# The local-attention mask as a ScalarE copy into PSUM, and K squared and rotated in two halves

## The chip, the cores and the metric

The kernel runs on one core of a Trainium2 chip. The metric is the device time of one execution in microseconds, as the median of several runs. TensorE appears in the profile as PE (its weight loads as PEld), VectorE as DVE, ScalarE as ACT, GpSimd as POOL and SyncE as SP. Arithmetic is float32 throughout, except for the mask products, which are bfloat16.

## The reference

The input x has 4 sequences of 512 tokens of width 128. First comes one global attention block with 16 heads of 64 (layer norm, causal penalty of -50, softmax, output product, residual). Then six layers follow, each made of a local attention and a feed-forward part, each with a residual. The part that matters here is the local attention of a layer:

```
qkv = shift_tokens(x) @ Wqkv             # 128 -> 3 x 1024
q = l2norm(q) * qs ; k = l2norm(k) * ksc
q = q*cos*scale + rotate_half(q)*sin*scale
k = k*cos/scale + rotate_half(k)*sin/scale
# windows of 32 queries; each sees its own 32 keys and the 32 before
mask = (it < jb) | (it > jb + w) | (jb == -1)
sim = where(mask, -max, 8 * q . k)
out = softmax(sim) @ v ;  return out @ Wo
```

The feed-forward part is a layer norm, a product of 128 to 2 x 341, a times GELU(gate), a product back to 128, with biases.

## The kernel before, in words

The program has two stretches. The first, to about 550 us, is the global attention; the change does not touch its work. The second handles the six layers as 96 **units** (6 layers x 4 sequences x 4 blocks of 128 tokens), and a **slot** per unit, in which three units are in progress at once: `u = unit(n)` gets its attention, `nxt = unit(n + 1)` its transposes, `new = unit(n + 2)` its projections, rotation and norms. The order of every engine's instructions is written out by hand in `slot` (L919); nothing is reordered, and each engine takes its own instructions in the order in which they stand there.

In a slot, in order of the program:

- `scores(u)` (L684): eight bfloat16 products of a 32-wide identity with the mask `band` (L690) start the two PSUM banks of the scores, 64 rows by 32 columns of the array each, 512 columns long. Then 64 small products q·k (L700; 128 matrix instructions, since a float32 product takes two passes) add to them. DVE takes the maximum (L710) and subtracts it (L712).
- The Q projection of `new` (L548), its square on ACT (L560); the exponentials of u on ACT (L718); for some slots a step of the layer norm; the output product of the unit before (L762); Q's rotation on DVE (L570, L576), added on POOL (L587).
- The K projection of `new` in two halves of 512 columns, each half in its own PSUM bank, between them the transposes of u's probabilities on PE (L661), each copied out by ACT (L664, pT). Then K's square on ACT in one instruction of 1024 columns (L560).
- `times_v(u, 0)` and `times_v(u, 1)` (L725): 32 small products each on PE (L737, 64 matrix instructions), then on DVE the division (reciprocal L746, product L747).
- K's rotation on DVE (L570, L576) and POOL's add (L587); the transpose of the output on DVE (L753); the sums of squares for Q and K (L565).
- `transpose_q(nxt)`: PE L661, ACT copies qT (L664). Then the V projection of `new` (L548), copied by ACT (L648, `keep_v`); `transpose_k(nxt)`: PE L661, ACT copies kT (L664).
- A step of the feed-forward part: two FFN products (L812, L813), a table load, GELU on ACT (L816), the gate on DVE (L820), or the closing product (L832, L835). Then the next slot's scores follow on PE. The inverse norms are taken on ACT and POOL (L590 to L603), and POOL applies them (L606).

The layer norm's and the feed-forward part's steps are spread over four slots each, so slots come in four kinds, by n modulo 4: without a norm step, with mean (L109), with variance (L118), with scale (L126). The feed-forward steps run from slot 7 on. In slots before that, K's transposes stand between the halves of the V projection. Once per 16 slots POOL also builds the rotation tables of a layer (L182).

PSUM for this stretch consists of three pairs of banks (`two_t`, L525), whose roles turn by one with every slot (`part[0] = -n % 3`), and two single banks (`one_t`). In a slot, pair 0 holds the scores, then the first half of PV, then V's projection; pair 1 holds Q's projection, then the second half of PV, then the FFN products; pair 2 holds K's projection, and turns into pair 0, the scores' pair, of the next slot. Squares and rotated products share four buffers (tag `t1`), the rotated vectors six (tag `rot`).

## Time and profile before

| what | us |
|---|---|
| median of 3 runs (lowest, highest) | 2070.51 (2067.06, 2072.57) |
| the profiled execution, its own time | 2072.4 |
| its span, first to last instruction | 2070.6 |
| PE busy | 2028.4 |
| DVE busy | 1640.8 |
| ACT busy | 1368.2 |
| POOL busy | 1316.5 |

The mean granted clock of TensorE is 0.996 of full speed. The engines run side by side, so their busy times do not add up; what counts is which engine is waited for. A line of the waits reads "engine and line waiting, engine and line waited for: us in total, times, longest". A line of the timeline reads "start, duration, engine, line of the code, operation, output <- inputs with their shapes, how many in a row", and in brackets the idle time ahead of it and who ended it. [...]

### The profile page before, as it was taken

The numbers are of one execution on the slowest core, as the hardware profiler recorded it, in microseconds if no ns is written. First come the engines' busy times: TensorE is split into PE (matmuls) and PEld (weight loads), VectorE is DVE, ScalarE is ACT, GpSimd is POOL, SyncE is SP. The second block draws the span as 40 slices with busy tenths as digits, with TensorE's granted clock in tenths as the row PEclk, the third lists the DMA queues.
The fourth block names the chain that finished last, engine by engine and source line by source line (L and its number), as shares of the span: only waits on it lengthen the run. The fifth ranks groups of instructions, "written<-read, shape, count | busy, mean of one in ns | idle before, by whom it ended". The sixth has DMA issues, their size and how long they took to land.

```text
span 2070.6 us, 77263 instructions
## 1 busy us (share of the span) xinstructions
PE 2028.4 (98%) x34382; PEld 1329.1 (64%) x34382; DVE 1640.8 (79%) x2240; ACT 1368.2 (66%) x2678; POOL 1316.5 (64%) x1432
## 2 busy tenths in 40 slices
PE   7999999999999999999999999999999999999998
PEld 5665555655466666666666666666666666666665
DVE  3766766767698888888888888888888888888885
ACT  3665665666455766676776676776667776677763
POOL 1554554555677677667767667667677767667762
PEclk8999999999999999999999999999999999999999
DMA  3000000000011121111211112111121111211110
GB/s 127 1 1 1 1 1 1 1 1 1 12 44 36 42 67 44 44 44 33 77 44 34 54 36 64 53 35 44 46 64 44 38 51 46 67 41 44 38 45 27
DMA packets 34968, 77.44 MB, mean 37 GB/s; under 512 B 4686, under 2 KB 18764, under 8 KB 34636
## 3 DMA queue, kind: packets, MB, share of 16 engines
q1 hardware_dynamic: 33932, 70.79, 11.8%
q8 instruction: 272, 4.46, 0.9%
q10 hardware_dynamic: 704, 1.70, 0.2%
q14 instruction: 60, 0.49, 0.1%
HBM read 23.50 MB, written 1.05 MB: 12 GB/s over the span
## 4 chain that ended last, share of the span: by engine, by line
PE 91%; DVE 5%; ACT 2%; POOL 1%; issue 1%; DMA 0%; SPq 0%; POOLq 0%; ACTq 0%
PE ps_proj L548 23%; PE ps_one L661 12%; PE ps_one L762 7%; PE ps_att L737 7%; PE ps_sc L308 6%; PE ps_o L393 6%; PE ps_att L700 5%; PE ps_pt L373 5%; PE ps_proj L812 3%; PE ps_proj L813 3%; PE ps_proj L832 3%; PE ps_pj L287 1%; PE ps_att L690 1%; PE ps_pj L277 1%; PE ps_pj L271 1%; PE ps_pj L407 1%
## 5 line engine op out<-in xcount | busy, mean ns | idle before, releaser
L587 POOL TENSOR_TENSOR rot<-rot,t 128x1024 f32<-128x1024 f32 x192 | 454.2, 2366 | 232.6 <-DVE t L576 220.1
L548 PE MATMUL ps_proj<-wqkv,xs 128*128 128x512 f32 x1152 | 569.0, 602 | 0.5 <-PE ps_one L661 0.2
L362 POOL TENSOR_TENSOR pr<-pr,den 128x1024 f32<-128x1024 f32 x128 | 241.0, 1893 | 248.3 <-DVE den L359 238.5
L606 POOL TENSOR_TENSOR rot<-rot,ss 128x1024 f32<-128x1024 f32 x192 | 361.3, 1903 | 7.4
L560 ACT ACTIVATE sq<-ps_proj 128x1024 f32<-128x1024 f32 x192 | 196.4, 1023 | 93.8 <-PE ps_proj L548 93.6
L548 PEld LDWEIGHTS ps_proj<-wqkv,xs 128*128 128x128 f32 x1152 | 188.2, 190 | 102.0 <-issue 92.1
L570 DVE TENSOR_TENSOR rot<-ps_proj,lt 128x1024 f32<-128x1024 f32 x192 | 233.3, 1215 | 10.2 <-ACT sq L560 10.0
L576 DVE TENSOR_TENSOR t<-ps_proj,lt 128x1024 f32<-128x1024 f32 x192 | 232.9, 1213 | 0.0
L348 ACT ACTIVATE pr<-ps_sc,nm 128x128 f32<-128x128 f32 (+3 forms) x448 | 220.3, 509 | 11.8 <-DVE nm L335 8.6
L565 DVE TENSOR_REDUCE ss<-sq 128x16 f32<-128x1024 f32 x192 | 221.1, 1190 | 0.0
L661 PEld LDWEIGHTS ps_one<-ident,rot 128*128 128x128 f32 x1536 | 172.7, 141 | 61.2 <-issue 51.2
L661 PE MATMUL ps_one<-ident,rot 128*128 128x128 f32 x1536 | 205.1, 276 | 1.1 <-POOL xs L170 0.6
L335 DVE TENSOR_REDUCE nm<-ps_sc 128x2 f32<-128x1024 f32 x128 | 155.9, 1218 | 62.9 <-PE ps_sc L323 62.8
L664 ACT COPY pT<-ps_one 128x512 f32<-128x512 f32 x192 | 110.0, 587 | 136.6 <-PE ps_one L661 136.6
L762 PEld LDWEIGHTS ps_one<-aT,wo 128*128 128x128 f32 x1536 | 182.9, 192 | 23.6 <-issue 17.7
L762 PE MATMUL ps_one<-aT,wo 128*128 128x128 f32 x1536 | 189.1, 276 | 0.3 <-ACT tmp_t L852 0.2
L746 DVE RECIPROCAL rden<-ps_att 128x8 f32<-128x8 f32 x192 | 38.8, 202 | 176.8 <-PE ps_att L737 176.7
L648 ACT COPY vt<-ps_proj 128x512 f32<-128x512 f32 x192 | 103.1, 590 | 96.4 <-PE ps_proj L548 96.4
L373 PEld LDWEIGHTS ps_pt<-ident,pr 128*128 128x128 f32 x1024 | 117.4, 142 | 58.5 <-issue 47.4
L664 ACT COPY qT<-ps_one 128x512 f32<-128x512 f32 x192 | 103.1, 589 | 66.1 <-PE ps_one L661 66.1
L377 ACT COPY pT<-ps_pt 128x512 f32<-128x512 f32 x128 | 75.6, 591 | 98.0 <-PE ps_pt L373 98.0
L373 PE MATMUL ps_pt<-ident,pr 128*128 128x128 f32 x1024 | 135.9, 274 | 3.0 <-DVE pT L381 2.4
(178 smaller groups left out, 3763.2 us busy)
## 6 DMA issues: line engine op xcount, KB each, us to landing
vs<-vt SPq DMA_DIRECT2D x96, 390.0 KB, 3.7
vs<-vt SPq DMA_DIRECT2D x72, 130.0 KB, 3.6
wqkv<-in_wqkv_dram SPq DMA_DIRECT2D x18, 512.0 KB, 4.0
vs<-in_zeros_dram SPq DMA_DIRECT2D x24, 130.0 KB, 3.7
wo<-in_wo_dram SPq DMA_DIRECT2D x6, 512.0 KB, 4.2
w<-in_w_dram SPq DMA_DIRECT2D x6, 341.0 KB, 5.9
xr<-in_x_dram SPq DMA_DIRECT2D x3, 256.0 KB, 7.6
scales<-in_scales_dram SPq DMA_DIRECT2D x6, 128.0 KB, 3.1
```

The costliest lines, as they stand in the source:

```text
L348: nc.scalar.activation(self.pr[:, h, cols], self.sc[:, h, cols], AF.Exp, bias=self.nm[:, part_, h : h + 1], accum_out=self.den[:, part_, h ...
L362: nc.gpsimd.tensor_tensor(self.pr, self.pr, self.den[:, 0].unsqueeze(2).to_broadcast([P, 2, S]), ALU.mult)
L373: nc.tensor.transpose(pt[:, k * P : (k + 1) * P], self.pr[:, h, k * P : (k + 1) * P], ident)
L548: mm(p[:, c, :], lhsT=u.xs[:, u.T * P : (u.T + 1) * P], rhs=wpart[j][:, c * 512 : (c + 1) * 512], start=True, stop=True,)
L565: nc.vector.tensor_reduce(u.ss[:, j * HEADS : (j + 1) * HEADS], heads(u.sq[j]), AX.X, ALU.add)
L570: nc.vector.tensor_tensor(heads(t0), heads(pf), lt[:, u.T, 2 * j].unsqueeze(1).to_broadcast([P, HEADS, HD]), ALU.mult)
L576: nc.vector.tensor_tensor(t1.rearrange("p (h t d) -> p h t d", t=2, d=half), pf.rearrange("p (h t d) -> p h t d", t=2, d=half)[:, :, ::-1, :],
L587: nc.gpsimd.tensor_tensor(u.r[j], u.r[j], u.t1, ALU.add)
L606: nc.gpsimd.tensor_tensor(heads(u.r[j]), heads(u.r[j]), u.ss[:, j * HEADS : (j + 1) * HEADS].unsqueeze(2).to_broadcast([P, HEADS, HD]), AL ...
L661: nc.tensor.transpose(tp[:, c * P : (c + 1) * P], src[:, (4 * g + c) * P : (4 * g + c + 1) * P], ident)
L664: nc.scalar.copy(dst[:, 4 * g : 4 * g + 4, col0 : col0 + P], tp.rearrange("p (c t) -> p c t", c=4))
L762: mm(y[:, 0:P], lhsT=wo_w[0][:, k, :], rhs=u.aT[:, g].rearrange("p (j f) -> p j f", f=P)[:, :, f0 : f0 + W], start=(k == 0), stop=(k == NC ...
```

## The change

For units 1 to 94 the mask no longer comes from products. At the end of the slot before, after the qT copies, ACT copies the mask (`mask`, a new float32 constant of 1 KB per partition, loaded at the start by one more DMA on SP's queue) into the pair of banks that K's projection has just left, broadcast over the eight chunks. The score products then add to it. Unit 0 and the last unit keep the products.

For that, K's banks must be read out earlier. In slots from 0 on, K's square is done in two halves of 512 columns, the first of them right behind the first half of K's projection, and K's rotation is done in halves as well: the first ahead of the first division, the second between the two divisions, where before it came after both. POOL's add for K follows the second half. `project` keeps K's pair of banks, unflattened, as `u.pk`.

```diff
+        nc.sync.dma_start(out=mask, in_=a["mask"])
         nc.sync.dma_start(out=tabs, in_=a["tabs"])
...
+    def square_half(u, c):
+        if c == 0:
+            u.sq[1] = s2a.tile([P, INNER], F32, tag="t1", name="sq", bufs=4)
+        nc.scalar.activation(u.sq[1][:, c * 512 : (c + 1) * 512], u.pk[:, c, :], AF.Square)
+
+    def rotate_half(u, c):
+        if c == 0:
+            u.r[1] = s2a.tile([P, INNER], F32, tag="rot", name="rot", bufs=6)
+            u.t1 = s2a.tile([P, INNER], F32, tag="t1", name="t1", bufs=4)
+        cols, lt, pf, half = slice(c * 512, (c + 1) * 512), u.lt, u.pk[:, c, :], HD // 2
+        nc.vector.tensor_tensor(
+            heads(u.r[1][:, cols]),
+            heads(pf),
+            lt[:, u.T, 2].unsqueeze(1).to_broadcast([P, HEADS // 2, HD]),
+            ALU.mult,
+        )
+        nc.vector.tensor_tensor(
+            u.t1[:, cols].rearrange("p (h t d) -> p h t d", t=2, d=half),
+            pf.rearrange("p (h t d) -> p h t d", t=2, d=half)[:, :, ::-1, :],
+            lt[:, u.T, 3].rearrange("p (t d) -> p t d", t=2).unsqueeze(1).to_broadcast([P, HEADS // 2, 2, half]),
+            ALU.mult,
+        )
...
+    def preset(u):
+        u.sc = two_t(2, "ps_att")
+        nc.scalar.copy(
+            u.sc.rearrange("p a (c n) -> p a c n", n=2 * W),
+            mask[:, min(u.T, 1)].unsqueeze(2).to_broadcast([P, 2, NC, 2 * W]),
+        )
+
     def scores(u):
-        sc = two_t(0, "ps_att")
-        for j, h, x_, p0 in PLACES:
+        sc = two_t(0, "ps_att") if u.sc is None else u.sc
+        for j, h, x_, p0 in PLACES if u.sc is None else ():
...
         if new:
             do_project(new, 1, 0, 1)
+            if n >= 0:
+                square_half(new, 0)
...
         if new:
             do_project(new, 1, 1)
-            square(new, 1)
+            if n == -1:
+                square(new, 1)
+            else:
+                rotate_half(new, 0)
+                square_half(new, 1)
...
         if u:
             times_v(u, 0)
+            if new:
+                rotate_half(new, 1)
+                add_rotated(new, 1)
             times_v(u, 1)
...
-        if new:
+        if new and n == -1:
             rotate(new, 1)
             add_rotated(new, 1)
...
         if nxt:
             transpose_q(nxt)
+        if new and n >= 0:
+            preset(nxt)
         if new:
             do_project(new, 2, 0, 2 if geglu else 1)
```

More of the change, by code (lines that the diff above doesn't have):

```diff
@@ L61, in body @@
     band = const.tile([P, 2, 2 * W], BF16, tag="band", name="band")
+    mask = const.tile([P, 2, 2, 2 * W], F32, tag="mask", name="mask")
     ident16 = const.tile([P, P], BF16, tag="ident16", name="ident16")
@@ L541, in __init__ @@
             self.i, self.b, self.T = i, b, T
-            self.r, self.sq = [None, None], [None, None]
+            self.r, self.sq, self.sc = [None, None], [None, None], None
     def project(u, j, c0=0, c1=2):
-        p = u.p[j] if c0 else two_t(((1, 2, 1), (0, 2, 1), (1, 2, 0))[min(u.n, 2)][j], "ps_proj")
+        p = (u.pk if j == 1 else u.p[j]) if c0 else two_t(((1, 2, 1), (0, 2, 1), (1, 2, 0))[min(u.n, 2)][j], "ps_proj")
         u.p[j] = p
+        if j == 1:
+            u.pk = p
         for c in range(c0, c1):
@@ L1141, in _constants @@
         band[r : r + W, 1] = np.where(seen, 0.0, NEG)
+    mask = np.repeat(band[:, 1:2, None, :], 2, 2).repeat(2, 1)
+    for r in range(0, P, HD):
+        mask[r + W : r + HD] = mask[r : r + W]
+        mask[r : r + W, 0, 0] = band[r : r + W, 0]
     band = band.astype(ml_dtypes.bfloat16)
@@ L1146, in _constants @@
     zeros = np.zeros((W, 2, NC, HD + 1), f)
-    return {"tabs": tabs, "band": band, "pen": pen, "ident16": ident16, "zeros": zeros}
+    return {"tabs": tabs, "band": band, "mask": mask, "pen": pen, "ident16": ident16, "zeros": zeros}
 def kernel(**inputs):
```

## The prediction

> **What bounds the kernel now.** I read the page's busy times and its chain first, then the waits, then the timeline of single slots, then the source lines of the mask products.

> ```profile
> PE 2028.4 (98%) x34382; PEld 1329.1 (64%) x34382; DVE 1640.8 (79%) x2240; ACT 1368.2 (66%) x2678; POOL 1316.5 (64%) x1432
> ...
> PE 91%; DVE 5%; ACT 2%; POOL 1%; issue 1%; DMA 0%; SPq 0%; POOLq 0%; ACTq 0%
> ```

> PE is busy 98% of the span, and 91% of the chain that ended last lies on it: a PE microsecond saved is worth one as long as nobody else becomes late. From the view of the waits:

> ```profile
> DVE rden L746 <- PE ps_att L737: 176.7, 98, 2.3
> ...
> ACT vt L648 <- PE ps_proj L548: 96.4, 95, 1.6
> ...
> PEld ps_one L661 <- ACT pr L718: 22.5, 35, 2.1
> ```

> The columns are total us, times, longest. DVE stands idle about 1.8 us (176.7/98) ahead of the first division of each slot, ACT about 1.0 us ahead of the V copies, both because PE is not there yet. PE itself waits for others mainly at one place, the transposes of the probabilities (L661), for the exponentials (L718).

> The timeline of one slot (start us, duration), the third of its group of four:

> ```profile
> 1207.03 1.02 PE L813 MATMUL ps_proj<-hT,w 128*85 128x512 f32 x2
> ...
> 1207.57 1.28 ACT L816 ACT_TABLE_LOAD   x1
> ...
> 1207.98 0.41 PE L690 MATMUL ps_att<-band,ident 64*32 64x512 bf16 x8
> ...
> 1208.21 1.46 PE L700 MATMUL ps_att<-kT,qT 64*32 64x64 f32 x128
> ...
> 1208.87 0.68 ACT L816 ACTIVATE tmp_t<-ps_proj,vecs 85x512 f32<-85x512 f32 x1
> ...
> 1209.58 0.75 DVE L820 SCALAR_TENSOR_TENSOR tmp_t<-ps_proj,vecs,tmp_t 85x512 f32<-85x512 f32 x1
> ...
> 1210.25 1.21 DVE L710 TENSOR_REDUCE mx<-ps_att 128x16 f32<-128x1024 f32 x1
> ...
> 1211.50 1.22 DVE L712 TENSOR_TENSOR pr<-ps_att,mx 128x1024 f32<-128x1024 f32 x1
> ...
> 1212.75 1.06 ACT L718 ACTIVATE pr<-pr 128x1024 f32<-128x1024 f32 x1
> ...
> 1214.10 0.60 PE L661 MATMUL ps_one<-ident,pr 128*128 128x128 f32 x4
> ...
> 1215.83 1.02 PE L548 MATMUL ps_proj<-wqkv,xs 128*128 128x512 f32 x2
> ...
> 1217.69 0.21 DVE L746 RECIPROCAL rden<-ps_att 128x8 f32<-128x8 f32 x1 [1.97 <-PE ps_att L737]
> ...
> 1218.92 1.07 ACT L664 COPY qT<-ps_one 128x512 f32<-128x512 f32 x2 [0.68 <-PE ps_one L661]
> ...
> 1221.08 1.07 ACT L648 COPY vt<-ps_proj 128x512 f32<-128x512 f32 x2 [1.08 <-PE ps_proj L548]
> ```

> Four things are to be seen: the eight mask products hold the score products back from 1207.98 to 1208.21; a serial chain runs from the V copies over table load, GELU, gate (L820), maximum, subtraction and exponentials to PE's transposes; DVE has a hole of 1.97 us before L746; ACT has one of 1.08 us before L648.

> **The change, part by part.**

> *Mask products off PE.* 94 of the 96 units (1 to 94) lose their eight products; unit 0 and the last keep them. From the first L690 to the first L700 it is 0.23 us; over all 96 slots of the trace the interval is 0.225 to 0.309 us and sums to 21.8 us. So 94/96 x 21.8 = 21.3 us go from PE. The 0.52 us between the starts of the last 128-row product and of the first L690 stays: PV products (L737), also in 64x32 tiles, stand 0.52 us behind L548 too.

> *Preset on ACT.* One copy of 128x1024 from SBUF into PSUM per slot. No row shows one. Bounds: 0.92 us (L560 to the next ACT start, 1228.06 to 1228.98) and 1.06 (mean of L718, SBUF to SBUF); I take 1.02, by L560 with the same shape between PSUM and SBUF. It stands behind the qT copies and ahead of V's, in the hole of 1.08 us that is there in all four kinds of slot. Two copies in a row overlap by about 0.1 us (two take 1.07 at 0.59 each), so it fits with 0.06 to 0.25 us over: cost nothing. Without that cover, V's copies and the chain behind them would come later by the excess. It also waits for DVE's last read of K's banks, below.

> *K by halves on ACT.* One 1.02 us square becomes two of 128x512: 0.59 (L664, same size) to 0.62 (L113). The second sits where the whole one did. The first comes before a pT copy: in the slot above K's first half is done for ACT at about 1215.60 (start of its second pass plus 0.63, as at 1216.26 to 1216.89), the half square runs to 1216.20, the copy that began at 1216.03 begins at about 1216.11, ends at 1216.70, and PE takes up PV at 1216.79: nothing. What queues behind it on ACT is the pT copy and then the second half square; PE waits for the copy, with 0.09 us left.

> *K by halves on DVE.* Two operations of 1.21 us (start to start 1.13) become four of 128x512 at 0.69 (L747, PSUM operand, same size), some 0.61 apart: 4 x 0.61 - 2 x 1.13 to 4 x 0.69 - 2 x 1.21, +0.18 to +0.34 us a slot, 17 to 32 us of DVE, none of it on the path. The first pair (1.30) starts after the first half square, 1216.26, and ends at 1217.56, ahead of the division at 1217.69; the four kinds of slot have holes of 1.56, 1.87, 1.97 and 2.02 us. The second pair starts when the first division's product (L747, 1217.93 to 1218.62) ends, and is through at 1219.84; ACT is free for the preset at 1219.9. The second division is 1.2 us later than now; its bank is next written by the FFN products, about 1 us later still. DVE then ends its sums of squares some 1.0 us earlier, but its next link, L820, waits for GELU, so this earns nothing in the steady slots. POOL's add for K starts earlier, with nobody waiting.

> *What is late next.* In the four kinds of slot the exponentials end ahead of PE's transposes by 0.25, 0.25, 0.29 and 0.06 us; where PE really waits (1261.49) the distance is 0.05. Slack is thus 0.20, 0.20, 0.24, 0.01. In the first three the chain begins at V's copies, before the mask products, and does not get shorter: 0.23 of PE time meets 0.20 of slack, so 0.03 comes back as waits in two kinds of slot, 48 x 0.03 = 1.4 us. In the fourth the chain starts at the Q projection, behind the scores, and moves with them: nothing. Once per 16 slots (table building on POOL, 5 times) PE already waits 0.8 us or more for a chain POOL-ACT two slots long (1244.48 to 1261.49); there both slots' 0.23 is lost: 5 x 0.45 = 2.3 us. In slots 1 to 7 there is no GELU and DVE itself is late; PE waits there beyond its usual spacing 3.2 us in all, and DVE's earlier end should give about 2 back.

> *Mask load.* One more transfer on SP's queue at about 16 us, ahead of the tables (L211, first used at 454.79): nothing.

> Sum: -21.3 + 1.4 + 2.3 - 2.0 = -19.6. Against the profiled execution (span 2070.6, 2072.4 with what lies around it) that is 2052.8; it stands 1.9 above the median of the runs, 2070.51, which gives **2051**.

> [...]

> **The rivals.**

> *K's second projection behind the half square (slower).* If the order is kept for K's whole tile and not for each bank, the product at 1215.83 waits for ACT's half square, 1216.20 plus 0.06: 0.43 us in three of four kinds of slot (in the fourth two transposes lie between). 70 x 0.43 = 30 us against 19.6: **2081**. It decides from 0.28 us per slot. For it: the trace of before has no reading of one half while the other is written. Against: the halves are separate banks, and the diff slices by bank everywhere.

> *ACT becomes late (about the same).* ACT gets 1.2 us per slot more, and the chain to the exponentials is serial through it. If preset or qT copies slip by 0.2 us past the hole (a slower write to PSUM, DVE's second pair late), three of four kinds of slot lose 0.2 us: 70 x 0.2 = 14, leaving **2065**. For: slack of only 0.06 by the longest price. Against: the overlap of 0.1 on ACT, and holes before each division.

> *More than forecast.* If DVE's earlier end also clears PE's waits for exponentials (22.5 + 8.0 us in two rows of waits, 5 us of it in the POOL cases), some 8 us more: **2043**. For: those waits exist. Against: in steady slots L820 waits for GELU.

> **How the numbers follow.** Forecast 0.70 (own range 2046 to 2058), ACT late 0.12, slower 0.11, more 0.07. The 0.3% that a measurement of this kernel can tell from no change is 6.2 us, so faster means under 2064.3, slower over 2076.7. ACT late lies on that bound and splits evenly; the slower rival gives a tenth of itself to the middle. Faster 0.83, same 0.07, slower 0.10. The range leaves out the slower rival and part of the ACT case: 2043 to 2066.

> **What would show it.** Right: L690 left with 16 products, the first L700 0.52 us behind the FFN's last start, 94 copies of some 1.0 us ahead of V's with almost no idle left there, DVE's wait before L746 down to some 0.1 to 0.5 us, the slot period down by about 0.2 us. Wrong: PE waiting at L548 for ACT's square (the slower rival), L648's start moved behind PE's V projection or the row L661 <- L718 grown beyond 40 us (ACT late), or half operations on DVE over 0.8 us.

## The result, and the profile after

The changed kernel takes 2121.14 us (median; 2118.75 to 2121.78), against 2070.28 us for the kernel before on the same chip: a ratio of 1.0239, 95% interval 1.0223 to 1.0255. It is 51 us slower where 20 us less were forecast. The profiled execution has a span of 2120.0 us at a granted clock of 0.995, after 0.996, so the clock has no part in it.

The page of the changed kernel, busy times and the chain that ended last:

```profile
PE 2044.5 (96%) x33630; PEld 1320.4 (62%) x33630; DVE 1663.1 (78%) x2428; ACT 1455.5 (69%) x2866; POOL 1319.3 (62%) x1432
...
PE 81%; ACT 7%; DVE 7%; POOL 3%; issue 2%; DMA 0%; SPq 0%; ACTq 0%; POOLq 0%
```

PE has 752 matrix instructions fewer, and its share of the chain falls from 91% to 81%: ACT and DVE have come onto the path. "Issue" stands at 2% where it was 1%. The line numbers have moved: K's and Q's projections are L552 now, the half square L569, the half rotation L576 and L582, PE's transposes L688 and their copies L691, the copy of the mask L715, V's copy L675, PV L773, the division L782 and L783. The waits of the changed kernel:

```profile
ACT sq L569 <- DVE t L582: 186.9, 94, 2.1
...
DVE rot L576 <- PE ps_proj L552: 130.7, 94, 1.8
...
PEld ps_proj L552 <- ACT sq L569: 33.6, 69, 0.5
...
PEld ps_one L688 <- ACT pr L754: 28.8, 35, 2.1
...
PE ps_proj L552 <- ACT sq L569: 17.2, 69, 0.3
```

All but the row L688 for L754 are new, and they form one chain (PE's products and its weight loads wait for the same half square): PE's second projection of K waits for ACT's half square of the first half, DVE's first half rotation waits for that projection, and ACT's second half square waits for the rotation. The old wait for the exponentials (L688 for L754) has grown only from 22.5 to 28.8 us. One slot in the timeline, the same kind as in the prediction:

```profile
1237.67 0.60 ACT L569 ACTIVATE sq<-ps_proj 128x512 f32<-128x512 f32 x1 [0.28 <-PE ps_proj L552]
...
1238.32 1.13 PE L552 MATMUL ps_proj<-wqkv,xs 128*128 128x512 f32 x2 [0.25 <-ACT sq L569]
...
1239.48 0.69 DVE L576 TENSOR_TENSOR rot<-ps_proj,lt 128x512 f32<-128x512 f32 x1 [1.72 <-PE ps_proj L552]
...
1240.87 0.60 ACT L569 ACTIVATE sq<-ps_proj 128x512 f32<-128x512 f32 x1 [2.12 <-DVE t L582]
...
1242.84 1.02 ACT L715 COPY ps_att<-mask 128x1024 f32<-128x1024 f32 x1
1243.79 1.06 ACT L675 COPY vt<-ps_proj 128x512 f32<-128x512 f32 x2
```

The half square of the first bank ends at 1238.27, and the projection into the *second* bank starts at 1238.32. The rotation of the first bank starts when the projection into the second has ended, and the square of the second bank waits 2.12 us for the rotation of the first. None of the three pairs touches a common bank: it looks as if the order were kept for K's whole tile.

To see where the time went, I divided PE's work from 560 us on into blocks, each from the first start of one kind of product to the first start of the next, and summed them. (Starts, as consecutive products overlap in the timeline: of the rows below, the product at 1323.16 lasts to 1323.37, and the next starts at 1323.31.) The wait ahead of K's second projection falls into the block of p's transposes.

| block, us in all | before | after | difference |
|---|---|---|---|
| band products | 21.6 | 0.5 | -21.1 |
| transposes of p, to the next projection | 89.4 | 120.7 | +31.3 |
| projections of Q, K, V | 507.3 | 520.4 | +13.1 |
| PV, and transposes of q and k | 316.0 | 338.8 | +22.8 |
| output product | 181.4 | 184.2 | +2.8 |
| scores, norm, FFN | 390.6 | 390.3 | -0.3 |

So the products went as forecast, and 70 us came in four other blocks. For the 22.8 us around PV there is no new row among the waits. In some slots of the changed kernel PE halts within PV and the transposes behind it; one such place:

```profile
1320.57 0.46 PE L773 MATMUL ps_att<-vs,pT 64*32 64x65 f32 x32
...
1321.54 0.53 PE L773 MATMUL ps_att<-vt,pT 64*32 64x65 f32 x30
...
1323.16 0.21 PE L773 MATMUL ps_att<-vt,pT 64*32 64x65 f32 x1 [1.10 <-issue]
1323.31 1.09 PE L688 MATMUL ps_one<-ident,rot 128*128 128x128 f32 x8
```

The product at 1323.16 is one of the same run of products; PE was idle for 1.10 us ahead of it, and nothing in the profile released it. One queue of the page bears on it, that of PE's instructions:

```profile
q8 instruction: 266, 4.36, 0.8%
```

The columns are packets, MB, share. 4.36 MB over 266 packets is 16 KB each, and PE's queue has 68,202 records in this trace, 256 to a packet. (Before, it was 272 packets for 69,699 records: also 256.) In the trace a packet begins at 1320.63 us, when PV has just begun, and has landed at 1321.62; PE goes on 1.5 us after that. Such halts recur some 32 or 65 us apart, mostly, in the kinds of slot with the mean and with the scale.

**Three theories** went into the experiments. **Theory 1**: the order per tile of K is the cause. **Theory 2**, its rival: the added operations cost by themselves, crowding ACT and DVE, and the waits are only where this shows. **Theory 3**: the halts in PV are instruction fetch. Without the 16 mask instructions per slot (eight products, each with its weight load) a group of four slots has 2558 or 2559 records on PE's queue, ten packets less one or two (2622 or 2623 before, about ten and a quarter), so that nearly the same instruction stands at a packet's end in every group.

### The profile page after: what moved, and what is told of

It is laid out like the page before. It is cut to its first block, busy times and chain, and to the rows that moved or that the text cites. A ratio compares the mean times of both kernels' runs of the same rounds, so it can differ in the third digit from the quotient of the medians.

```text
span 2120.0 us, 76338 instructions
## 1 busy us (share of the span) xinstructions
PE 2044.5 (96%) x33630; PEld 1320.4 (62%) x33630; DVE 1663.1 (78%) x2428; ACT 1455.5 (69%) x2866; POOL 1319.3 (62%) x1432
## 3 DMA queue, kind: packets, MB, share of 16 engines
q8 instruction: 266, 4.36, 0.8%
## 4 chain that ended last, share of the span: by engine, by line
PE 81%; ACT 7%; DVE 7%; POOL 3%; issue 2%; DMA 0%; SPq 0%; ACTq 0%; POOLq 0%
PE ps_proj L552 21%; PE ps_one L688 10%; PE ps_one L798 6%; PE ps_sc L310 6%; PE ps_o L395 6%; PE ps_att L773 5%; PE ps_att L736 5%; PE ps_pt L375 5%; PE ps_proj L868 3%; PE ps_proj L848 2%; PE ps_proj L849 2%; ACT sq L569 2%; POOL rot L614 2%; PE ps_pj L289 1%; PE ps_pj L279 1%
## 5 line engine op out<-in xcount | busy, mean ns | idle before, releaser
L552 PE MATMUL ps_proj<-wqkv,xs 128*128 128x512 f32 x1152 | 580.6, 612 | 17.7 <-ACT sq L569 17.2
L552 PEld LDWEIGHTS ps_proj<-wqkv,xs 128*128 128x128 f32 x1152 | 188.0, 190 | 138.4 <-issue 91.4
L569 ACT ACTIVATE sq<-ps_proj 128x512 f32<-128x512 f32 x188 | 112.3, 597 | 210.7 <-DVE t L582 186.9
L576 DVE TENSOR_TENSOR rot<-ps_proj,lt 128x512 f32<-128x512 f32 x188 | 129.0, 686 | 130.7 <-PE ps_proj L552 130.7
L688 PEld LDWEIGHTS ps_one<-ident,rot 128*128 128x128 f32 x1536 | 173.1, 141 | 78.5 <-issue 65.2
L688 PE MATMUL ps_one<-ident,rot 128*128 128x128 f32 x1536 | 209.0, 277 | 12.1 <-issue 8.1
L798 PEld LDWEIGHTS ps_one<-aT,wo 128*128 128x128 f32 x1536 | 182.9, 192 | 23.5 <-issue 17.2
L691 ACT COPY pT<-ps_one 128x512 f32<-128x512 f32 x192 | 109.7, 585 | 60.3 <-PE ps_one L688 59.6
L564 ACT ACTIVATE sq<-ps_proj 128x1024 f32<-128x1024 f32 x98 | 100.0, 1022 | 60.9 <-PE ps_proj L552 58.9
L783 DVE TENSOR_TENSOR on<-ps_att,rden 128x512 f32<-128x512 f32 x192 | 132.8, 692 | 6.6
L310 PEld LDWEIGHTS ps_sc<-k,q 64*128 64x128 f32 x1024 | 94.4, 189 | 66.7 <-issue 30.0
L310 PE MATMUL ps_sc<-k,q 64*128 64x256 f32 x1024 | 130.9, 395 | 4.7 <-ACT pr L350 3.0
```

Source lines behind the costliest of these rows:

```text
L310: mm(sc[:, h, k0 : k0 + S // 2], lhsT=qs[b, c][rows, t * P : (t + 1) * P], rhs=ks[b, c][rows, k0 : k0 + S // 2], start=(k0 == 0), stop=Fal ...
L552: mm(p[:, c, :], lhsT=u.xs[:, u.T * P : (u.T + 1) * P], rhs=wpart[j][:, c * 512 : (c + 1) * 512], start=True, stop=True,)
L569: nc.scalar.activation(u.sq[1][:, c * 512 : (c + 1) * 512], u.pk[:, c, :], AF.Square)
L688: nc.tensor.transpose(tp[:, c * P : (c + 1) * P], src[:, (4 * g + c) * P : (4 * g + c + 1) * P], ident)
L798: mm(y[:, 0:P], lhsT=wo_w[0][:, k, :], rhs=u.aT[:, g].rearrange("p (j f) -> p j f", f=P)[:, :, f0 : f0 + W], start=(k == 0), stop=(k == NC ...
```

## The experiments

Times are medians; the kernel before ran beside them at 2069.9 to 2071.1 us. Ratios are to it.

**1. The half square behind the second projection.**

```diff
             do_project(new, 1, 0, 1)
-            if n >= 0:
-                square_half(new, 0)
...
             else:
+                square_half(new, 0)
                 rotate_half(new, 0)
                 square_half(new, 1)
```

> The changed kernel with one move: the first half square of K is issued behind K's second projection instead of ahead of it; nothing is left out. Theory 1 (the order between engines is kept per tile of K, so the second projection waits for ScalarE's half square of the first half): the waits of the second projection for L569 in the changed kernel, 33.6 us on the weight loads and 17.2 us on the products (some 69 slots), go, and with them the 0.41 us that these slots lose ahead of it: 2121 less 29 to 37 us, 2084 to 2092 us. Theory 2 (the added half operations and the copy cost by themselves, by crowding ScalarE and VectorE): the same operations are still there and ScalarE is later with them, 2115 to 2130 us. Theory 3 (TensorE's instruction fetch stands still in the slots whose position modulo the 256-instruction packets is fixed) says nothing of this edit: its some 22 us of stalls in the products with V stay under either.

Measured: 2121.74 us, ratio 1.0246 (1.0230 to 1.0261), the same as the changed kernel. My number missed, and theory 2's was met. Experiment 2 decides between the theories; but the waits already speak against theory 2's mechanism, for DVE and ACT stand idle in them:

```profile
DVE rot L576 <- ACT sq L569: 155.2, 94, 1.9
...
ACT sq L569 <- DVE t L582: 127.4, 94, 1.4
...
PE ps_proj L552 <- DVE on L783: 38.0, 83, 0.6
```

PE's wait ahead of K's second projection is gone (transposes of p from 120.7 to 93.0 us), but now the readers hold each other up: DVE's first half rotation waits for the half square, which has come later, and ACT's second half square for the rotation. The first of these two orders lies within one bank, and experiment 2 keeps it (31.6 us there, 69 times); only the second is between banks. The rotation stands ahead of the division of PV's first half, and V's projection, which takes over that half's banks, waits for that division. The blocks of PV and the transposes of q and k go from 338.8 to 372.6 us. The wait moved; it was not removed.

**2. No order between the two banks.** The program is told that the three pairs of instructions share no bytes; nothing is moved.

```diff
             k_mm = mm(
...
+            if j == 1 and c == 1 and u.sq0 is not None:
+                tc.declare_no_dep(k_mm.ins, u.sq0.ins, reason="other bank")
...
+            for r in u.rh:
+                tc.declare_no_dep(f.ins, r.ins, reason="other bank")
...
+            for r in u.rh:
+                tc.declare_no_dep(r.ins, u.kmm[1].ins, reason="other bank")
```

Here `f` is the second half square, `u.rh` the two half rotations of the first bank, `u.kmm[1]` the second projection.

> The changed kernel with the orders between K's two banks taken out: the second projection no longer waits for the half square of the first bank, the rotation of the first bank no longer for the second projection, and the second half square no longer for the rotation of the first bank. Nothing is left out and nothing is moved. Theory 1: all waits that come from keeping the order for the tile go, those of TensorE (0.41 us in some 70 slots, 29 us, and 8 us within the projection) and those that make ScalarE late (the second half square waits for VectorE): 2070 to 2085 us with the fetch stalls of theory 3 still there. It lies below the kernel with the square moved behind. Theory 2: the same operations cost the same, 2110 us or more.

Measured: **2052.85 us, ratio 0.9915 (0.9898 to 0.9932)**: faster than both kernels, and 68 us below the changed one. Theory 1 holds and theory 2 falls: the same operations are all still there, and PE's queue has the same 68,202 records, so that the places in the packets are the same too. A slot of the kind above:

```profile
1205.15 0.60 ACT L574 ACTIVATE sq<-ps_proj 128x512 f32<-128x512 f32 x1 [0.28 <-PE ps_proj L553]
1205.39 1.02 PE L553 MATMUL ps_proj<-wqkv,xs 128*128 128x512 f32 x2
...
1205.78 0.69 DVE L586 TENSOR_TENSOR rot<-ps_proj,lt 128x512 f32<-128x512 f32 x1 [0.53 <-ACT sq L574]
...
1206.45 0.60 ACT L574 ACTIVATE sq<-ps_proj 128x512 f32<-128x512 f32 x1 [0.22 <-PE ps_proj L553]
...
1207.24 0.21 DVE L796 RECIPROCAL rden<-ps_att 128x8 f32<-128x8 f32 x1 [0.17 <-PE ps_att L787]
...
1209.44 1.04 ACT L729 COPY ps_att<-mask 128x1024 f32<-128x1024 f32 x1
...
1210.63 1.07 ACT L689 COPY vt<-ps_proj 128x512 f32<-128x512 f32 x2 [0.16 <-PE ps_proj L553]
```

Square and projection overlap, the rotation fits into DVE's hole ahead of the division (0.17 us of it are left), the copy of the mask into ACT's ahead of V's copy (0.16 left). It came out lower than I had expected, since the halts in PV went as well: PV and both transposes take 315.3 us, after 338.8. That they hang on the orders too was not foreseen; experiments 3 to 6 follow it.

**3. A shift of 64 instructions**, and **4. both together.** In unit 0's scores, once:

```diff
+        for _ in range(4 if u.n == 0 else 0):
+            for j, h, x_, p0 in PLACES:
+                rows = slice(h * HD, (h + 1) * HD)
+                mm(
+                    sc[p0 : p0 + W, x_, 0:1],
+                    lhsT=ident16[rows, h * HD : h * HD + W],
+                    rhs=band[rows, 1, W : W + 1],
+                    start=False,
+                    stop=False,
+                    skip_group_check=True,
+                )
```

> The changed kernel with 64 one-column products more in the first unit of attention, once (they add zero): every later instruction of TensorE stands a quarter of a 256-instruction packet further on. Theory 3 (a group of four slots has exactly ten packets after the change, so that the same instructions stand at a packet's end in every group, and they stand where TensorE has used up what was fetched): the some 22 stalls of 0.7 to 1.5 us without a releaser go or move, 2121 less up to 22 us, some 2100 us. Rival (these stalls belong to something else, as the wait for a buffer or the work they stand in): same places, same sizes, 2119 to 2123 us. Theory 1 and 2 expect nothing of it.

> Both edits together: no order between K's two banks, and 64 one-column products more in the first unit. Theories 1 and 3 together: the two parts add, 2121 less 37 to 50 us less up to 22 us, 2050 to 2065 us, below the kernel before. Theory 1 alone (the stalls stay): as the kernel without the orders, 2070 to 2085 us. Theory 2: 2110 us or more.

Measured: the changed kernel with the shift, 2106.30 us, ratio 1.0172 (1.0155 to 1.0189), 14.8 us less, from 32 matrix products added once: with their weight loads they are the 64 instructions (the text above calls them 64 products). PV with the transposes of q and k falls by 22.2 us to 316.6; 4.5 us come back in the projections; no row of the waits shows why. So the halts do belong to the place in the packet. Both edits together, 2055.28 us, ratio 0.9927 (0.9911 to 0.9943): in the range, but the parts do not add. Without the orders there was nothing left for the shift to take.

**5. A shift of 128**, half a packet (`range(8 ...)` in place of `range(4 ...)`, 64 products), and **6. the same without the orders.**

> The changed kernel with 128 one-column products more in the first unit, once (they add zero): every later instruction of TensorE stands half a 256-instruction packet further on, so that the slots whose products with V began at places 181 to 194 of a packet (where the changed kernel stalls) now begin them at 53 to 66, and the other slots the other way round. Theory 3 (the stall belongs to the place in the packet together with the wait that holds TensorE's queue ahead of K's second projection): the stalls leave the kinds of slot that had them and appear in the other kind with that wait; the kind of slot without the norm step, which has no such wait, stays free of them. So about half of them are left: 2121 less some 7 us, 2109 to 2117 us. Rival 3a (the place alone decides): all of them move, 2118 to 2123 us. Rival 3b (any disturbance of the count clears them): as with 64, 2104 to 2108 us.

> The kernel without the orders between K's banks, and 128 one-column products more in the first unit (they add zero). The shift by 128 moved the stalls of the changed kernel to the other kinds of slot, the one without the norm step among them, and cleared none. Theory 3 with the wait (a slot stalls where the packet's place lets the fetch begin with the products with V, and it begins that late only where a wait has held TensorE's queue just ahead): no stalls here, 2050 to 2057 us, the fetches ahead of the products with V in these slots beginning 0.5 to 1 us earlier than they do. Rival (the place alone decides, and the kernel without the orders has only been lucky with its two places): stalls in the slots that begin the products with V at places 184 to 190, 2060 to 2075 us.

Measured: 2133.65 us, ratio 1.0310 (1.0292 to 1.0328), and 2067.24 us, ratio 0.9985 (0.9975 to 0.9994). Both main expectations missed. With the orders, the halts moved to the other two kinds of slot, the kind without a norm step among them, as rival 3a had it, and the total was above all three numbers. Without the orders, the time lies in the range of the rival, that the place alone decides; but the halts appear in one of the two kinds only, which that rival doesn't explain. The traces sort it. For slots 8 to 91 that begin PV at places 175 to 200 of a packet, when does the fetch begin that falls there, and how many take over 2.7 us from PV's first product to the first weight load of V's projection (2.27 to 2.35 is usual)?

| kernel | kind of slot at these places | fetch begins, against PV's start (median) | over 2.7 us |
|---|---|---|---|
| after | mean; scale | +0.10; +0.07 | 24 of 31 |
| 5: shift of 128 | no norm step; variance | -0.10; +0.05 | 28 of 34 |
| 2: no orders | mean; scale | -0.66; -0.94 | 2 of 31 |
| 6: no orders, shift of 128 | no norm step | -0.42 | 10 of 17 |
| 6: no orders, shift of 128 | variance | -0.95 | 0 of 17 |
| 3 and 4: shift of 64 | none at these places | | 0 |

A fetch takes 0.88 to 1.46 us in the changed kernel (266 fetches), and PV's 256 instructions are used up in 1.3 us. Over the changed kernel and kernels 2, 5 and 6, of the 46 slots of this table whose fetch begins 0.6 us or more ahead of PV 3 take over 2.7 us; of the 67 whose fetch begins 0.2 us ahead of PV or later 56 do. When it begins goes with a wait just ahead: the record of the semaphore instruction for PV's wait, the last before PV, lies 1.06 us ahead of PV in the changed kernel, behind the held projection, and 1.63 to 2.14 us ahead without the orders; the kind without a norm step has the shortest of these, 1.63. Why the two go together, no run shows.

**7 and 8. The orders one at a time.** Kernel 7 has only the first of the three declarations of experiment 2, so that PE's order alone is out; kernel 8 has only the other two.

> The changed kernel with one of the three orders between K's banks taken out, that of TensorE: K's second projection no longer waits for the half square of the first bank. VectorE's first half rotation still waits for the second projection, ScalarE's second half square still for that rotation. Nothing is left out. The kernel without any of the three took 2053 us. Theory 1a (only TensorE's own wait costs, the 0.41 us ahead of the projection, the 0.11 us within it and the fetch stalls that the held queue brings): 2053 to 2058 us. Theory 1b (the order also makes ScalarE late with q's copies, as in the kernel with the square moved behind, where TensorE then lost 0.64 us in front of V's projection in most slots): between, 2065 to 2100 us.

> The counterpart of the kernel that lost TensorE's order alone (2074 us): here that order is kept (K's second projection waits for the half square of the first bank) and the other two are taken out. Nothing is left out. Without all three it took 2053 us. Theory 1: the wait costs its 0.41 us in some 70 slots and 0.11 us within the projection, 29 to 37 us, and up to 15 us of fetch stalls since the queue is held again: 2082 to 2105 us. Rival (the three orders only cost together, through ScalarE being late): 2053 to 2070 us, without the wait for L569's square ahead of the projection.

Measured: 2074.04 us, ratio 1.0017 (1.0007 to 1.0027), and 2110.05 us, ratio 1.0193 (1.0177 to 1.0209). Theory 1b holds for the one; the other lies 5 us above theory 1's range. As a square:

| us | PE's order out | PE's order kept |
|---|---|---|
| the other two out | 2052.85 | 2110.05 |
| the other two kept | 2074.04 | 2121.14 |

PE's order alone costs 57 us: against kernel 2 the transposes of p take 28.1 us more, PV and the transposes of q and k 21.2 (halts in 21 of 31 slots at those places), the projections 7.3. The row of the wait is the same as in the changed kernel, in kernel 8's lines:

```profile
PEld ps_proj L553 <- ACT sq L572: 33.7, 69, 0.5
```

The other two alone cost 21 us, in blocks 11.4 in the projections, 7.9 in the transposes of q and k, 2.8 in the output product, with DVE's first half rotation waiting 102.3 us in all for the projection; beside PE's order they cost 11.

**9 and 10. The halves without the copy**, with the orders and without them. In `slot`:

```diff
-        if new and n >= 0:
-            preset(nxt)
```

> The halves of the change without its copy of the mask: the band's products stay in the scores as in the kernel before, K is squared and rotated by halves as in the changed kernel. The output is complete. Theory 1 (the order kept per tile of K costs, the copy does not): the kernel before plus 0.41 and 0.11 us in some 70 slots, 2071 plus 29 to 37 us, 2100 to 2108 us; the wait for L569 ahead of K's second projection is there as in the changed kernel. Rival (the copy of the mask makes ScalarE late and so brings the waits): near the kernel before, 2065 to 2080 us, and no such wait.

> Halves without the orders between the banks, and without the copy of the mask: the band's products stay. The output is complete. If the halves cost nothing once the banks are free of each other: as the kernel before, 2066 to 2074 us, and the difference to the kernel with the copy and without the orders (2053 us) is what the copy is worth, 17 to 21 us by the forecast's 94/96 of 21.8 us less its small terms. Rival (the halves free VectorE early and give time by themselves, the copy little): 2053 to 2062 us.

Measured: 2118.04 us, ratio 1.0224 (1.0209 to 1.0239), and 2067.39 us, ratio 0.9982 (0.9973 to 0.9992). So the halves bring the loss without any copy of the mask, 10 us more of it than the upper number (transposes of p +28.7, projections +13.1, PV and transposes +7.4 against before), and without the orders they cost nothing, they earn 3.7 us (2071.1 beside them). The copy is then worth 14.5 us (2067.39 to 2052.85), below the 17 to 21 expected: 6.0 us come back in the transposes of p and the output product. In the changed kernel it was worth nothing (2118.04 to 2121.14): its 21 us went into PV and the transposes of q and k (+15.4), the output product (+5.4) and the transposes of p (+2.6); by the count above it is the copy, which takes 64 instructions out of a group, that holds the place in the packet: the changed kernel begins PV at places 175 to 200 in 31 of the 84 slots, kernel 9 in 11.

**11. The copy without the halves.**

```diff
-                rotate_half(new, 0)
-                square_half(new, 1)
+            square(new, 1)
...
-        if new and n == -1:
+        if new:
             rotate(new, 1)
             add_rotated(new, 1)
```

> The copy of the mask alone: the band's products are gone, K is squared and rotated as a whole in the places of the kernel before. The output is complete. No half square stands between K's two projections, so theory 1 expects no wait for ScalarE there. The copy takes its PSUM tile where K's rotation has let it go, some 1.6 us later in ScalarE's queue than in the changed kernel, with V's and k's copies behind it. If the slack that k's copy has before the scores (some 1 us in the kernel before) covers most of it: 2053 to 2075 us, and the halves would not have been needed. If not, 0.5 us and more in 94 slots: 2095 to 2140 us.

Measured: 2166.33 us, ratio 1.0458 (1.0442 to 1.0473), above both expected ranges. The kind of slot above, in its timeline:

```profile
1242.29 1.22 DVE L603 TENSOR_TENSOR t<-ps_proj,lt 128x1024 f32<-128x1024 f32 x1
...
1243.59 1.02 ACT L715 COPY ps_att<-mask 128x1024 f32<-128x1024 f32 x1 [1.81 <-DVE t L603]
...
1244.54 1.07 ACT L675 COPY vt<-ps_proj 128x512 f32<-128x512 f32 x2
...
1245.50 1.09 ACT L691 COPY kT<-ps_one 128x512 f32<-128x512 f32 x2
...
1246.15 1.48 PE L736 MATMUL ps_att<-kT,qT 64*32 64x64 f32 x128 [0.74 <-ACT kT L691]
```

The copy waits 1.81 us for the end of K's rotation, which frees its banks, and holds V's and k's copies back until PE waits for k. The earlier rotation was thus needed for the copy, and only its order per tile made it dear.

## Why the prediction was wrong, point by point

- **The products off PE, -21.3 us**: right, 21.1 to 21.4 in the blocks of every kernel that has the copy.
- **The prices**: the copy at 1.02 us (1.02 to 1.04 measured), the half square at 0.59 to 0.62 (0.60), the half rotation at 0.69 (0.69): right. So were the holes that were to hide them, once the orders are gone: kernel 2 has the picture of the prediction, with 0.17 us left ahead of the division and 0.16 ahead of V's copy.
- **The step that failed is "K by halves on ACT"**: "What queues behind it on ACT is the pT copy and then the second half square; PE waits for the copy, with 0.09 us left." It took each half to be free when its own bank is, and so put the half square's cost to PE at nothing. The runs show that PE waits for the half square itself, some 0.4 us in 69 slots, and that this one order costs 57 us (2110.05 against 2052.85), halts in PV included. **"K by halves on DVE"** failed by the same assumption: the first pair "starts after the first half square, 1216.26, and ends at 1217.56, ahead of the division"; it starts behind the second projection and holds the division back.
- **The rival that named it**, K's second projection behind the half square, was right in mechanism and place, and wrong in size and in its chance. Its 0.43 us a slot was met (28 to 31 us in the block, 30 by its sum). It left out what came in other blocks, 38 us against kernel 2: 23.5 in PV and the transposes of q and k, most of it halts (kernel 3 takes 22.2 out of these blocks), and 12.7 in the projections and 2.1 in the output product (PE's order alone brings 7.3 in the projections; the other two alone 11.4 there and 2.8 in the output product). So it said 2081 where 2121 came. I gave it 0.11 on the argument that the halves are separate banks and that the code slices by bank. But the code allocates one tile for both, and the trace of before speaks for the rival at a place that I did not read for it. In the FFN, L812 writes the first bank of a pair and L813 the second; the GELU (L816) reads the first alone. Late in the program ACT stands idle ahead of it:

```profile
2048.05 1.02 PE L812 MATMUL ps_proj<-hT,w 128*128 128x512 f32 x2
...
2048.91 1.02 PE L813 MATMUL ps_proj<-hT,w 128*128 128x512 f32 x2
...
2049.97 0.69 ACT L816 ACTIVATE tmp_t<-ps_proj,vecs 128x512 f32<-128x512 f32 x1 [0.79 <-PE ps_proj L813]
```

The first bank's product ends at 2049.07, the second's at 2049.93, and the GELU starts at 2049.97: it waits for the bank that it does not read. So the order for the whole tile stood in the trace, and the rival deserved the larger chance.
- **The small terms, +1.4 + 2.3 - 2.0**: kernel 2 shows them. Its span is 18.6 us below before's, forecast 19.6. The block of p's transposes, where PE's waits for the exponentials lie, grows by 2.9 us (3.7 forecast); slots 1 to 7 become 4.6 us shorter, 7 x 0.23 = 1.6 of which are the products, so 3.0 for DVE's earlier end (2.0 forecast).

## What to carry to other kernels

When an operation is split so that a reader comes between two writes of one allocation, look in the trace for a reader of one part that waits for the writer of the other, as the GELU does here (0.79 us), and price the order for the whole allocation unless the trace shows a finer one. Then state that the pairs share nothing, which here turned +51 us into -18, or give each bank its own tile (not tried here). And in experiment 1 moving an instruction that waits to another place moved the wait with it (2121.74 us, after 2121.14): look at what the waiting order is made of before moving anything.
